# A GpSimd iota between one indirect DMA and the next, in a graph layer with segment maximum

## The chip, the cores and the metric

The kernel runs on one core of a Trainium2 chip. A core has five engines with instruction streams of their own: TensorE (PE in the profile; its weight loads are PEld), VectorE (DVE), ScalarE (ACT), GpSimd (POOL) and SyncE (SP), which here only issues DMAs. They meet at semaphores. All DMAs of the core, whoever issues them, are carried out by its 16 DMA engines. The metric is the device time in microseconds of one execution, lower is better.

## The reference

There are 6250 nodes with 256 features (`x`) and 100,000 edges, each with a source and a destination; the edges come sorted by destination. With the linear maps theta and phi, an edge from s to d has

```python
theta_x = (x_dst - x_src) @ theta_w.T + theta_b
phi_x = x_src @ phi_w.T + phi_b
e = jax.nn.relu(theta_x + phi_x)
out = jax.ops.segment_max(e, dst, num_segments=x.shape[0])
```

A node without edges gets 0. Then `x + out` is normalised over the 256 features: mean taken off, divided by the root of variance + 1e-5.

The maps can be taken apart: the edge's value is A(d) + B(s), with A = x theta_w.T and B = x (phi_w - theta_w).T + both biases. A depends on the destination alone, so a node needs the maximum of B over its sources, and then max(A + that, 0). What remains is matrix work on 6250 rows and, for every edge, the fetching of a row of B (1 KB) and a maximum.

## The kernel before, in words

The nodes are cut into two parts. Part 1 is the first 2154 nodes, part 2 the last 4096 (32 tiles of 128).

*B.* At the start x is loaded in 13 pieces, transposed on TensorE (L669), copied out on ScalarE (L671), multiplied (L675), the bias added on VectorE (L678), and the rows of B are stored to `b_rows` in HBM by DMAs on ScalarE's queue (L693).

*Part 1, by gathers.* Its edges are laid on 128 partitions in chunks of 275. In step t a gather fetches, for each partition, the row of B of that chunk's edge t: one indirect DMA on GpSimd of 128 rows of 1 KB, with its 128 offsets in a column in SBUF. Eight steps make a group with a tile `g` of its own; a ring of seven such tiles (`RING = 7`) lets GpSimd run ahead. VectorE runs through a group's steps (L722): the maximum of the new row with the former one, the former capped to minus infinity where a new node begins. SyncE then stores the group to `maxima_1` (L726). Five of the first groups (`of_x`) gather rows of x instead, while B is not ready, and multiply them on the spot. There are 35 groups, 40 + 235 gathers.

*Part 2, by matmuls in parts ("chunks").* B's rows are cut in 17 slots of up to three blocks of 125 rows. For each slot and each of four chunks of 1024 nodes, at most one source per node and slot is chosen on VectorE (`choice`). A part of (slot, chunk) then loads the wanted row numbers from HBM (L945, SyncE), makes one-hot matrices from them on VectorE (L949) and ScalarE (L951, L952), multiplies them with the slot's rows, split in two float32r terms (L934, L935), on TensorE into PSUM (L959, 24 matmuls of 128 x 512 for a whole part), and VectorE takes the maximum into `acc` (L970; in the first slot ScalarE copies, L968). There are 68 parts. To find a node's sources, 33 short gathers (L475) fetch 640 destinations and then, for each of 32 tile columns, 36 sources a partition; these come early and need what ScalarE counts at L628 and VectorE turns into `begin_i` (L632).

*The left-over list.* Edges of part 2 that no slot took are squeezed into a list of 240 steps (`list_pieces`, L980 to L1040) and gathered as in part 1: 30 groups, 240 gathers, the same ring, L722 and a store to `maxima_2`.

*The end.* `rows_of` gathers the maxima by place (49 gathers), loads x, computes A on TensorE (L1071 to L1077), takes the maximum with `acc` for part 2 (L1086, L1087), adds and applies relu (L1088, L1091); `normalise` squares and scales on ScalarE (L1104, L1111) and stores.

*What sets the order.* The order is written out by hand in the code. Each engine works through its instructions in this order and waits where a semaphore isn't there yet. After two groups for each pair of slots, and a stretch in which the list is squeezed, the loops issue a group of gathers and then 1.2 parts (`PACE`), so the stream of VectorE mixes the L722 steps of gathered groups with L949 and L970 of parts. Between the two lists stands `heads_1`, which repairs the first rows of the chunks with two indirect DMAs (L832, L834) that wait for the stores of part 1.

All gathers but those two go through two helpers:

```python
    def gather(to, table, offsets):
        nc.gpsimd.indirect_dma_start(
            out=to, out_offset=None, in_=table, in_offset=bass.IndirectOffsetOnAxis(ap=offsets, axis=0)
        )
```

`gather` is L467, its DMA L468; `gather_run` is L472, its DMA L475. The helper `iota(t, step, base, per_partition)` (L458, L459) writes an arithmetic sequence along the columns of a tile on GpSimd.

Of the kernel before, what the change touches and what calls it, by code (L numbers as in the profile page):

```python
# [36 lines left out]
FP = mybir.dt.float32  # L37
# [11 lines left out]
P = 128  # L49
# [14 lines left out]
SLOT = 512  # L64
DVE_HOTS = 1
PACE = 1.2
LOWEST = -1.0e30
ABSENT = 1 << 14
MAGIC = 12582912.0
# [8 lines left out]
def flat(t, offset, ap):  # L78

    return bass.AP(tensor=t.tensor, offset=t.offset + offset, ap=ap)  # L80
# [325 lines left out]
def gnn_kernel(ctx: ExitStack, tc: tile.TileContext, x, src, dst, theta_w, theta_b, phi_w, phi_b, out):  # L406
# [27 lines left out]
    const = ctx.enter_context(tc.tile_pool(name="const", bufs=1))  # L434
# [23 lines left out]
    def iota(t, step, base, per_partition):  # L458
        nc.gpsimd.iota(  # L459
            t,  # L460
            pattern=[[step, t.shape[1]]],
            base=base,
            channel_multiplier=per_partition,
            allow_small_or_imprecise_dtypes=True,
        )

    def gather(to, table, offsets):  # L467
        nc.gpsimd.indirect_dma_start(  # L468
            out=to, out_offset=None, in_=table, in_offset=bass.IndirectOffsetOnAxis(ap=offsets, axis=0)
        )  # L470

    def gather_run(to, table, offsets):  # L472

        n = to.shape[1]
        nc.gpsimd.indirect_dma_start(  # L475
            out=to,
            out_offset=None,
            in_=flat(table, 0, [[n, EDGES // n], [1, n]]),
            in_offset=bass.IndirectOffsetOnAxis(ap=offsets, axis=1),
        )  # L480


    src_1 = const.tile([P, T1], I32, name="src_1")
# [6 lines left out]
    def gather_group(i, table):  # L490
        t0, n = groups[i]
        if i not in ring_tiles:
            ring_tiles[i] = gathered.tile([P, STEPS, D], FP, name="g")
        for k in range(n):
            gather(ring_tiles[i][:, k, :], table, src_1[:, t0 + k : t0 + k + 1])
# [75 lines left out]
    lowest_rows = search.tile([P, 2 * D], FP, name="lowest_rows")  # L571
    nc.vector.memset(lowest_rows, LOWEST)
    nc.sync.dma_start(maxima_1[NONE_1 : NONE_1 + 1, :], lowest_rows[0:1, :D])
# [35 lines left out]
    index = body.enter_context(tc.tile_pool(name="index", bufs=1))  # L609
    dst_w = index.tile([P, WINDOW], I32, name="dst_w")  # L610
    gather_run(dst_w, dst_list, edge0_i)
    for i in of_x[X_BEFORE:]:
        gather_group(i, x)
# [10 lines left out]
    for j0 in range(0, TILES + 1, BATCH):  # L624
        j1 = min(j0 + BATCH, TILES + 1)
        for j in range(j0, j1):
            junk = index.tile([P, WINDOW], BF, name="junk")
            nc.scalar.activation(  # L628
                junk, local, AF.Sign, bias=halves[:, j : j + 1], scale=-1.0, accum_out=sums[:, j : j + 1]
            )  # L630
        nc.vector.tensor_scalar(begin[:, j0:j1], sums[:, j0:j1], 0.5, 0.5 * WINDOW, op0=ALU.mult, op1=ALU.add)
        nc.vector.tensor_scalar(begin_i[:, j0:j1], begin[:, j0:j1], edge0, None, op0=ALU.add)  # L632
        for j in range(j0, min(j1, TILES)):
            gather_run(table_i[:, j, :], src_list, begin_i[:, j : j + 1])
# [127 lines left out]
    def node_place(j):  # L762
        cols = columns[:, j // Q1, :]
        hot = work.tile([P, P], FP, name="hot_1")
        nc.vector.tensor_scalar(hot, cols, low[:, j : j + 1], None, op0=ALU.is_ge)
        nc.vector.scalar_tensor_tensor(hot, cols, high[:, j : j + 1], hot, op0=ALU.is_lt, op1=ALU.mult)
        pp = misc()
        nc.tensor.matmul(pp[:, : T1 + 2], hot, ids_1[:, 1:], start=True, stop=True)
        for i in range(2):
            junk = work.tile([P, T1], BF, name="junk_1")  # L770
            nc.scalar.activation(
                junk, pp[:, :T1], AF.Sign, bias=upper[:, i, j : j + 1], scale=-1.0, accum_out=signs[:, i, j : j + 1]
            )
        nc.scalar.copy(origin[:, j : j + 1], pp[:, T1 + 1 : T1 + 2])
# [147 lines left out]
    raw = slots.tile([P, KB, D], FP, name="raw", bufs=1)  # L922
    nc.vector.memset(raw, LOWEST)
    terms_of = {}
# [119 lines left out]
    def group_2(t0):  # L1044
        g = gathered.tile([P, STEPS, D], FP, name="g")
        for k in range(STEPS):
            gather(g[:, k, :], b_rows, list_src[:, t0 + k : t0 + k + 1])
        run(2, g, STEPS, caps_2, t0, maxima_2t)


    def rows_of(part, tiles, ps_tile):
# [11 lines left out]
        for k, j in enumerate(tiles):  # L1063
            gather(m[:, k, :], maxima, places[:, j : j + 1])
# [77 lines left out]
    while groups_1:  # L1142
        group_1(groups_1.pop(0))
        if todo:
            node_place(todo.pop(0))
        pace += PACE
        while pace >= 1.0:
# [13 lines left out]
    while lists:  # L1161
        group_2(lists.pop(0))
        pace += PACE
        while pace >= 1.0:
# [61 lines left out]
```

## Time and profile before

| | |
|---|---|
| time, median of 3 runs | 1137.29 us (1129.62 to 1144.01) |
| profiled execution | 1127.47 us, span 1125.6 us |
| mean granted TensorE clock | 0.788 |
| gathers of the 256-feature rows (L468) | 235 + 240 + 49 + 40, mean 1184, 986, 961, 964 ns |
| short gathers (L475) | 33, 944 ns |
| POOL busy | 640.3 us |
| DVE busy | 630.7 us, of which L722 244.3 and L970 155.5 |
| PE busy | 651.4 us, of which L959 444.9 |
| DMA | 195.61 MB, mean 174 GB/s |

The durations come from one profiled execution. A row of the timeline gives start and duration in us, the engine, the line, the operation, out<-in, how many were merged, and in brackets how long the engine stood idle before and what ended that. A row of waits gives who waited for whom, us in total, how many times, and the longest. "issue" means that the engine waited for nothing that the profile shows; "remote" means that the semaphore was raised by something that the profile could not name. Matmul ends are modelled. [...] The row of a stage gives, for each engine, busy us and the number of instructions, then the granted clock, the mean busy share of the DMA engines and GB/s.

### The profile page before, as it was taken

How to read it: one execution, taken by the hardware profiler on the slowest of the kernel's cores; microseconds unless marked ns; L12 is line 12 of the kernel's file. 1: busy time of each engine (PE TensorE's matmuls, PEld its weight loads, DVE VectorE, ACT ScalarE, POOL GpSimd, SP SyncE). 2: the span in 40 equal slices, each digit the busy share in tenths (PEclk: the TensorE clock that was granted, in tenths of full speed). 3: DMA queues.
4: the chain of work that ended last, by engine and by line, in shares of the span. 5: the costliest groups of instructions: out<-in, count | busy, mean ns of one | idle time of the engine just before them, and what ended most of it. 6: DMA issues, size and time to landing. Idle time of an engine off the chain costs nothing. (4 is left out here: it accounts for less than half of the span.)

```text
span 1125.6 us, 9291 instructions
## 1 busy us (share of the span) xinstructions
PE 651.4 (58%) x2557; PEld 503.6 (45%) x2557; DVE 630.7 (56%) x1309; ACT 429.2 (38%) x680; POOL 640.3 (57%) x622
## 2 busy tenths in 40 slices
PE   0466893585147403295829328578185785986273
PEld 0355783364135302173607216456164664764262
DVE  1221693799978621184758118276165584994164
ACT  0256220564114210075655105276254463830175
POOL 6735377488888777554524754667555756204500
PEclk9888996787668756596959757889586977988696
DMA  6445365477455645264738627566275665735222
GB/s 213 128 138 165 113 193 179 140 254 238 169 173 190 201 144 166 77 221 128 229 122 290 188 81 226 165 220 213 85 238 182 219 202 189 240 144 215 80 99 92
DMA packets 63082, 195.61 MB, mean 174 GB/s; under 512 B 14071, under 2 KB 22795, under 8 KB 53515
## 3 DMA queue, kind: packets, MB, share of 16 engines
q1 hardware_dynamic: 32207, 112.01, 28.3%
q0 software_dynamic: 28272, 75.14, 23.2%
q10 hardware_dynamic: 2540, 7.75, 1.8%
q8 instruction: 23, 0.38, 0.1%
q14 instruction: 40, 0.33, 0.1%
HBM read 114.27 MB, written 81.38 MB: 174 GB/s over the span
## 5 line engine op out<-in xcount | busy, mean ns | idle before, releaser
L959 PE MATMUL ps_f<-hot,terms 128*128 128x512 f32 x1600 | 444.9, 436 | 293.7 <-DVE hot L949 123.0
L959 PEld LDWEIGHTS ps_f<-hot,terms 128*128 128x128 f32 x1600 | 334.6, 213 | 392.5 <-issue 222.9
L468 POOL DMA_INDIRECT g<-b_rows,src x235 | 278.3, 1184 | 118.1 <-issue 67.7
L468 POOL DMA_INDIRECT g<-b_rows,list_src x240 | 236.6, 986 | 148.2 <-issue 72.3
L970 DVE TENSOR_TENSOR acc<-acc,ps_f 128x1024 f32<-128x1024 f32 x128 | 155.5, 1215 | 252.5 <-remote 228.7
L951 ACT ACTIVATE hot<-want,minus_row 128x1024 fp32r<-128x1024 f16 x132 | 146.1, 1145 | 323.3 <-remote 200.3
L722 DVE SCALAR_TENSOR_TENSOR g<-g,caps 128x256 f32<-128x256 f32 x513 | 244.3, 478 | 27.5 <-DMA g<-b_rows,src 9.7
L952 ACT ACTIVATE hot<-hot 128x1024 fp32r<-128x1024 f32 x132 | 133.9, 1050 | 0.4
L675 PE MATMUL ps_b<-weights,x_t 128*128 128x256 f32 x356 | 94.1, 421 | 55.0 <-ACT x_t L671 43.0
L468 POOL DMA_INDIRECT g<-maxima,place x49 | 47.1, 961 | 109.3 <-issue 62.0
L675 PEld LDWEIGHTS ps_b<-weights,x_t 128*128 128x128 f32 x356 | 72.9, 211 | 73.5 <-ACT x_t L671 48.2
L1077 PE MATMUL ps_e<-weights,x_t 128*128 128x256 f32 x128 | 37.4, 440 | 39.2 <-ACT x_t L1073 37.3
L671 ACT COPY x_t<-ps_xt 128x512 f32<-128x512 f32 (+1 forms) x45 | 24.9, 577 | 76.3 <-remote 31.1
L949 DVE TENSOR_SCALAR hot<-want,row_id 128x1024 fp32r<-128x1024 f16 x68 | 50.9, 748 | 1.3 <-ACT hot L952 1.3
L475 POOL DMA_INDIRECT table_i<-src_list,begin_i x32 | 30.2, 944 | 34.0 <-DVE begin_i L632 24.5
L468 POOL DMA_INDIRECT g<-in_x_dram,src x40 | 38.5, 964 | 15.9 <-issue 11.3
L1077 PEld LDWEIGHTS ps_e<-weights,x_t 128*128 128x128 f32 x128 | 25.9, 213 | 47.1 <-ACT x_t L1073 41.2
L678 DVE TENSOR_TENSOR b_sb<-ps_b,bias 128x512 f32<-128x512 f32 (+1 forms) x25 | 16.7, 677 | 52.3 <-PE ps_b L675 22.9
L1104 ACT ACTIVATE squares<-g,r 128x256 bf16<-128x256 f32 x49 | 24.3, 498 | 47.7 <-issue 39.8
L628 ACT ACTIVATE junk<-local,halves 128x640 bf16<-128x640 f32 x33 | 27.4, 830 | 32.1 <-DVE b_sb L678 16.3
L1087 DVE TENSOR_TENSOR g<-g,ps_e 128x512 f32<-128x512 f32 (+1 forms) x17 | 11.1, 655 | 48.7 <-PE ps_e L1086 23.7
L1073 ACT COPY x_t<-ps_e 128x512 f32<-128x512 f32 (+1 forms) x17 | 9.4, 553 | 61.0 <-PE ps_e L1071 38.3
(194 smaller groups left out, 511.1 us busy)
## 6 DMA issues: line engine op xcount, KB each, us to landing
maxima<-g SPq DMA_DIRECT2D x64, 1024.0 KB
want<-chosen_rows SPq DMA_DIRECT2D x68, 256.0 KB
x_q<-in_x_dram SPq DMA_DIRECT2D x12, 512.0 KB
b_rows<-b_sb ACTq DMA_DIRECT2D x12, 512.0 KB
raw<-b_rows SPq DMA_DIRECT2D x16, 336.0 KB
g<-in_x_dram SPq DMA_DIRECT2D x5, 1024.0 KB
out_dram<-g SPq DMA_DIRECT2D x5, 1024.0 KB
g<-b_rows,list_src POOLq DMA_INDIRECT x240
```

Of the source, the lines that this page charges most:

```text
L468: nc.gpsimd.indirect_dma_start(out=to, out_offset=None, in_=table, in_offset=bass.IndirectOffsetOnAxis(ap=offsets, axis=0))
L475: nc.gpsimd.indirect_dma_start(out=to, out_offset=None, in_=flat(table, 0, [[n, EDGES // n], [1, n]]), in_offset=bass.IndirectOffsetOnAxis ...
L628: nc.scalar.activation(junk, local, AF.Sign, bias=halves[:, j : j + 1], scale=-1.0, accum_out=sums[:, j : j + 1])
L671: nc.scalar.copy(x_t[:, :n], ps[:, :n])
L675: nc.tensor.matmul(ps[:, i, :], x_t[:, i, k, :], weights[:, 1, k, :], start=(k == 0), stop=(k == KC - 1))
L722: nc.vector.scalar_tensor_tensor(g[:, k, :], last[part], caps[:, t : t + 1], g[:, k, :], op0=ALU.min, op1=ALU.max)
L949: nc.vector.tensor_scalar(hot[:, b, :], want, row_id[:, b : b + 1], None, op0=ALU.is_equal)
L951: nc.scalar.activation(hot[:, b, :], want, AF.Abs, bias=minus_row[:, b : b + 1], scale=1.0)
L952: nc.scalar.activation(hot[:, b, :], hot[:, b, :].bitcast(FP), AF.Relu, bias=1.0, scale=-1.0)
L959: nc.tensor.matmul(ps[:, w : w + 512], terms[:, part, b, h * P : (h + 1) * P], hot[:, b, w : w + 512], start=(i == 0), stop=(i == n - 1),)
L970: nc.vector.tensor_tensor(to, to, ps, op=ALU.max)
L1077: nc.tensor.matmul(a[:, i, :], x_t[:, 2 * i + c, :], weights[:, 0, c, :], start=(c == 0), stop=(c == KC - 1))
```

## The change

A tile of 128 x 144 float32 of its own, `pause`, is made in SBUF. Behind the indirect DMA in each of the two helpers GpSimd fills it with 0, 1, 2, ... 143 in every partition. Nothing reads it. The two indirect DMAs of `heads_1` are outside the helpers and get no iota behind them.

```diff
+PAUSE = 144
...
+    pause = const.tile([P, PAUSE], FP, name="pause")
+
     def gather(to, table, offsets):
         nc.gpsimd.indirect_dma_start(
             out=to, out_offset=None, in_=table, in_offset=bass.IndirectOffsetOnAxis(ap=offsets, axis=0)
         )
+        iota(pause, 1, 0, 0)
 
     def gather_run(to, table, offsets):
 
@@ -478,6 +483,7 @@
             in_=flat(table, 0, [[n, EDGES // n], [1, n]]),
             in_offset=bass.IndirectOffsetOnAxis(ap=offsets, axis=1),
         )
+        iota(pause, 1, 0, 0)
```

## The prediction

> **What bounds the kernel now.** I read the page's totals first, then the table by stages, then the timelines of GpSimd and TensorE in one stage, then the waits.
>
> ```profile
> span 1125.6 us, 9291 instructions
> PE 651.4 (58%) x2557; PEld 503.6 (45%) x2557; DVE 630.7 (56%) x1309; ACT 429.2 (38%) x680; POOL 640.3 (57%) x622
> ```
>
> No engine is near full, and the busy shares hide two things. The first is in the timeline of GpSimd:
>
> ```profile
> 465.80 0.95 POOL L468 DMA_INDIRECT g<-b_rows,src  x1 [0.30 <-issue]
> 467.06 0.94 POOL L468 DMA_INDIRECT g<-b_rows,src  x1 [0.30 <-issue]
> 468.30 0.95 POOL L468 DMA_INDIRECT g<-b_rows,src  x1 [0.30 <-issue]
> 488.23 1.71 POOL L468 DMA_INDIRECT g<-b_rows,src  x1 [18.98 <-DVE hot L766]
> ```
>
> A gather counts 0.95 us as busy, but the next starts 1.25 us after it: each has 0.30 us of its own that is not counted. With it GpSimd's 597 gathers hold the engine for about 640 + 597 x 0.30 = 820 us of 1126. From 143 to 977 us (493 gathers, 834 us) it stands still for only about 150 us beyond these gaps, waiting for VectorE, as in the last line, or for a store. So GpSimd is the nearest thing to a bound.
>
> The second: in the table by stages (time, then busy time and number of instructions of PE, PEld, DVE, ACT, POOL; clock; DMA share; GB/s) TensorE almost stops in some stretches.
>
> ```profile
> 230.00:290.00 60.00, 41.61 (x158) 31.99 (x156) 58.70 (x137) 31.66 (x36) 49.33 (x36) 0.84 0.72 246
> 395.00:415.00 20.00, 0.00 (x0) 0.00 (x0) 0.02 (x1) 0.00 (x0) 15.13 (x16) 0.50 0.48 157
> 452.00:470.00 18.00, 6.04 (x12) 3.47 (x12) 0.51 (x2) 0.00 (x0) 13.24 (x14) 0.50 0.36 103
> 488.00:507.00 19.00, 18.55 (x81) 14.67 (x79) 15.28 (x29) 11.92 (x21) 14.61 (x14) 1.00 0.78 257
> 507.00:522.00 15.00, 4.26 (x8) 1.82 (x8) 0.32 (x1) 3.79 (x8) 9.55 (x10) 0.64 0.39 114
> 980.00:1000.00 20.00, 17.95 (x78) 14.51 (x77) 19.75 (x32) 12.47 (x12) 0.00 (x0) 0.98 0.54 201
> ```
>
> The DMA engines are not full there (share 0.36 to 0.48, less than where TensorE runs well). What is special is that gathers follow each other every 1.25 us. TensorE's timeline shows the change within one such stretch:
>
> ```profile
> 499.09 5.83 PE L959 MATMUL ps_f<-hot,terms 128*128 128x512 f32 x24
> 511.60 0.59 PE L959 MATMUL ps_f<-hot,terms 128*128 128x512 f32 x1 [1.73 <-issue]
> 514.43 0.59 PE L959 MATMUL ps_f<-hot,terms 128*128 128x512 f32 x1 [0.82 <-issue]
> ```
>
> 24 matmuls take 5.83 us, 0.24 us each; after some 16 gathers in close order one starts every 1.4 us, and it waits for nothing that the profile shows. I call this the crawl. It ends when GpSimd pauses: the last gathers before GpSimd's waits ended at 469.2, 519.4, 667.7, 809.5 and 953.4 us; VectorE got its PSUM tile at 476.9, 522.9, 674.2, 813.7 and 952.2 (the next at 957.2), mostly 3.5 to 7.5 us later. VectorE pays:
>
> ```profile
> DVE acc L970 <- remote: 228.7, 21, 24.4
> POOL g L468 <- DVE g L722: 44.5, 9, 13.1
> POOL g L468 <- DVE hot L766: 37.1, 3, 19.0
> ```
>
> So the middle works in turns: gathers fill the ring of seven tiles while TensorE and VectorE crawl; the ring is full and GpSimd stops; the others catch up; the gathers go on.
>
> **The change.** It removes and moves nothing. It adds 597 iotas of 128 x 144 f32 on GpSimd (564 behind L468, 33 behind L475; none behind the two at L832 and L834), no DMA, no buffer that others use. An iota waits for nobody; behind it on GpSimd stands the next gather, and for that VectorE (L722).
>
> *What one costs.* The nearest rows:
>
> ```profile
> 23.88 0.18 POOL L459 IOTA halves<- 128x33 f32 x1
> 23.99 0.63 POOL L459 IOTA columns<- 128x128 f32 x3
> 24.57 0.23 POOL L459 IOTA ids<- 128x1 f32 x2
> 124.06 0.35 POOL L459 IOTA local<- 128x240 f32 x1
> ```
>
> From start to start 33 columns took 0.11 us and 128 took (24.57 - 23.99) / 3 = 0.193, so 0.0009 us a column and 0.21 us for 144. The high end is the last row, an iota that follows a gather: 0.35 for 240, less 96 columns, 0.27. The low end is zero, if it fits under the 0.30 us gap. Against that: begin_i (L632) ends at 70.40 and the gather that waited for it starts at 70.67. The gap comes after the wait too, so it is the gather's own preparation and runs in series. I take 0.21: a gather every 1.46 us.
>
> *What it should bring.* Where gathers came more slowly, TensorE did not crawl: 36 in 60 us from 230 to 290 (one per 1.67 us) with VectorE full, 14 in the 19 us from 488 (one per 1.36) with TensorE full, but crawling in the 15 us after it (one per 1.25 at the end). I read that as a backlog that fills after 15 to 30 us of gathers at 1.25 to 1.35 us and drains in a few us. Two stretches size it: crawl after about 16 us at 0.8 gathers per us (488 to 507, the ones after 605 and 822 similar) and after about 30 us at 0.74 (143 to 174) give a drain of about 0.68 per us, a limit near 1.47 us. That is an estimate from two points. With 1.46 us, and longer where VectorE delays gathers (the gathers of part 1 took 1184 ns in the mean, 0.95 us where nothing delays them), I expect the crawl mostly gone, though with no margin.
>
> *A rule against it.* The Trainium skill, SBUF — State Buffer, section "Who interferes with whom", says "PE and ACT never wait on anyone", and that nothing on the engines' side contends but VectorE and GpSimd. By it the crawl isn't caused by gathers, the pause buys nothing, and the sum is 1127 plus the pause (rival 1). The rows above, with one matmul per 1.4 us while GpSimd issues and 0.24 us when it doesn't, speak for the link, though not for what carries it; I follow the rows. The same section says that GpSimd and a VectorE operation in a two-port mode exclude each other for the whole instruction. An iota then blocks VectorE at most 0.21 us, in a seventh of the time (0.21 of 1.46): if half of VectorE's 991 instructions of the middle were of that kind, 500 x 0.14 x 0.1 = 7 us, on an engine with over 200 us of idle time. I put in 5 us for both directions together.
>
> *The sum*, against the profiled execution's 1127.47 us (span 1125.6):
> - 0 to 143 us: 33 gathers stand ahead of the one for dst_w, whose landing VectorE awaits for 13.3 us, until 52.16: 33 x 0.21 = +7. In return VectorE's wait of 9.5 us for b_sb, which ended 3.9 us after the last of these gathers, should shrink. The bundles of eight for table_i (+1.7 each) lie under waits for begin_i, but for the last. Together +3. Without the cover: +9.
> - 143 to 977 us: GpSimd's work is 834 - 150 = 684 us. The pauses add 493 x 0.21 = 104. Of the waits I keep 20: the row pass for heads (23.4, 4.1 and 3.5 us at L832 to L834, about 12 when VectorE isn't late) and stores that must land (12.3, about 8). With 5 for the port: 684 + 104 + 20 + 5 = 813, so -21. Late next is GpSimd itself; VectorE has about 510 us of work in it and TensorE about 490.
> - 977 to 1126 us: 24 gathers in close order from 1025.8 cost 24 x 0.21 = +5; ScalarE's wait until 1064.2, again a crawl, should lose about 10. Together -5.
>
> 1127.5 + 3 - 21 - 5 = 1104. The profiled execution lies 10 us below the median of 1137.29 and near the fastest run; I leave the forecast on its basis.
>
> **The rivals.**
> 1. *Slower: the crawl stays as long as gathers run, whatever their pitch.* Then the ring fills more slowly, the others crawl all that time, and the catching-up afterwards is as long as now: + 104 + 7 + 5, 1243; if waits take up a third of the 104, 1208. I take 1210. For it: the crawl is tied to GpSimd being busy at all, which the iota only increases, the rule above, and that at 1.33 to 1.4 us it did come, only later. Against it: the stretch 230 to 290. It decides against the change where less than about 110 of the 150 us of waits disappear.
> 2. *Half: 1.46 us is at the limit, the crawl comes later and lasts shorter.* About 75 us of waits stay in place of 20: 1104 + 55 = 1159.
> 3. *The pause is hidden in the gap* and nothing changes: pitch 1.25, crawl as before, 1120 to 1140, about 1130. Against it the 0.27 us after L632.
>
> **The numbers.** Forecast 0.53 (1104, own range 1065 to 1140: 0.27 us a pause adds 30, no waits at all and a cheaper pause take 35 off), rival 1 0.22 (1165 to 1245), rival 2 0.15 (1135 to 1180), rival 3 0.10. Two per cent of 1137.29, about what a measurement of this kernel can tell, puts the borders at 1114.5 and 1160. Faster by more: about 0.8 of the first case, 0.42. Slower: most of rival 1 and half of rival 2, 0.29. Between: 0.29. The range 1065 to 1205 leaves out the upper half of rival 1 and the tails.
>
> **What would show it.** In the changed profile the gather rows should be 1.46 us apart with iotas of about 0.25 us between; VectorE's wait for acc should fall from 229 to under 60 us; GpSimd's waits for VectorE from over 100 to under 20; TensorE's clock should rise in the middle, since it no longer idles. GpSimd's idle time after 222 us tells the cases apart: near nothing is the forecast, over 100 us is rival 1, a pitch of 1.25 is rival 3. The forecast is wrong if the crawl depends on GpSimd's being busy rather than on gathers per time, or if the iota costs more than 0.27 us next to a gather.

## The result and the profile after

The changed kernel takes 1261.01 us in the median (4 runs, 1258.77 to 1263.68) against 1140.65 us for the kernel before (4 runs, 1129.62 to 1158.63): 1.109 times as long, 95% interval 1.100 to 1.118. Slower by a tenth, where 1104 us was forecast with a range up to 1205.

The page of the changed kernel opens so; the last two lines are groups (busy time and mean ns of one, idle time before it and what ended most of that):

```profile
span 1257.0 us, 9882 instructions
PE 661.6 (53%) x2557; PEld 509.3 (41%) x2557; DVE 636.2 (51%) x1309; ACT 430.3 (34%) x680; POOL 778.7 (62%) x1219
...
L976 DVE TENSOR_TENSOR acc<-acc,ps_f 128x1024 f32<-128x1024 f32 x128 | 155.4, 1214 | 266.5 <-remote 206.8
L460 POOL IOTA pause<- 128x144 f32 x597 | 165.6, 277 | 38.0 <-DMA g<-in_x_dram,src 1.0
```

The iotas are there, 597 of them at 0.28 us, and no other engine has more instructions than before. (Lines after the helpers are six higher: L976 is L970 of the kernel before, L472 and L480 are L468 and L475.) GpSimd's timeline shows what the forecast had not considered:

```profile
105.21 13.07 POOL L460 IOTA pause<- 128x144 f32 x41
...
149.27 21.43 POOL L460 IOTA pause<- 128x144 f32 x55
...
198.84 10.97 POOL L460 IOTA pause<- 128x144 f32 x34
...
219.04 0.95 POOL L472 DMA_INDIRECT g<-b_rows,src  x1 [0.30 <-issue]
220.29 1.58 POOL L472 DMA_INDIRECT g<-b_rows,src  x1 [0.30 <-issue]
221.88 7.49 POOL L460 IOTA pause<- 128x144 f32 x21
```

**The iotas do not stand between the gathers.** Only among the gathers of x at the start does one follow one. Then come 26, 34, 41 and 32 iotas ahead of the four bundles of eight gathers for `table_i`, 68 more ahead of the first gather of part 1, and 10 to 34 between groups of eight gathers that still follow each other every 1.25 us. After 520 us none is left, and the crawl is back as it was. Three rows of TensorE's timeline, then VectorE's longest waits in 0 to 520 us, then the longest in 520 to 1257 us:

```profile
738.20 7.74 PE L965 MATMUL ps_f<-hot,terms 128*128 128x512 f32 x29
746.18 0.40 PE L965 MATMUL ps_f<-hot,terms 128*128 128x512 f32 x1 [0.24 <-issue]
763.65 3.73 PE L965 MATMUL ps_f<-hot,terms 128*128 128x512 f32 x8 [17.07 <-issue]
```

```profile
DVE g L728 <- issue: 67.7, 15, 8.3
DVE g L728 <- DMA g<-b_rows,src: 54.5, 35, 10.6
DVE source L860 <- DMA table_i<-src_list,begin_i: 38.9, 1, 38.9
```

```profile
DVE acc L976 <- remote: 206.8, 17, 24.0
```

Before 520 us no wait of VectorE for `acc` on something unnamed is left. In the first 534 us of the kernel before this was VectorE's longest:

```profile
DVE acc L970 <- remote: 85.6, 5, 24.4
```

In its place VectorE waits for gathered rows (L728; 9.7 us on that DMA before) and for `table_i` (2.7 us before). After 520 us all 206.8 us of the crawl's wait are there.

The gathers' landmarks, first to last start, of the kernel before and then of the changed one:

```profile
L468 POOL DMA_INDIRECT g<-b_rows,src x235: 942/947/7447, 143.0 to 534.3; - x118
```

```profile
L472 POOL DMA_INDIRECT g<-b_rows,src x235: 942/949/2721, 177.3 to 644.3; - x118
```

So of the 131 us between the two spans 34 arise before part 1, 76 in it (391 to 467 us), and 21 behind it, where no iota stands. For those 21 us I have no reason; the kernel before alone spread over 29 us in its four runs.

### The profile page after: what moved, and what is told of

The parts are those of the page before. It is cut to its first block, busy times and chain, and to the rows that moved or that the text cites. A ratio compares the mean times of both kernels' runs of the same rounds, so it can differ in the third digit from the quotient of the medians.

```text
span 1257.0 us, 9882 instructions
## 1 busy us (share of the span) xinstructions
PE 661.6 (53%) x2557; PEld 509.3 (41%) x2557; DVE 636.2 (51%) x1309; ACT 430.3 (34%) x680; POOL 778.7 (62%) x1219
## 5 line engine op out<-in xcount | busy, mean ns | idle before, releaser
L965 PE MATMUL ps_f<-hot,terms 128*128 128x512 f32 x1600 | 453.6, 441 | 414.9 <-DVE hot L955 144.7
L472 POOL DMA_INDIRECT g<-b_rows,list_src x240 | 238.1, 992 | 172.8 <-issue 72.0
L728 DVE SCALAR_TENSOR_TENSOR g<-g,caps 128x256 f32<-128x256 f32 x513 | 244.7, 479 | 136.3 <-issue 72.2
L472 POOL DMA_INDIRECT g<-b_rows,src x235 | 250.3, 1065 | 95.9 <-issue 75.7
L976 DVE TENSOR_TENSOR acc<-acc,ps_f 128x1024 f32<-128x1024 f32 x128 | 155.4, 1214 | 266.5 <-remote 206.8
L460 POOL IOTA pause<- 128x144 f32 x597 | 165.6, 277 | 38.0 <-DMA g<-in_x_dram,src 1.0
L472 POOL DMA_INDIRECT g<-maxima,place x49 | 47.2, 964 | 110.8 <-DMA maxima<-g 52.5
L1083 PE MATMUL ps_e<-weights,x_t 128*128 128x256 f32 x128 | 40.7, 471 | 36.9 <-ACT x_t L1079 36.2
L472 POOL DMA_INDIRECT g<-in_x_dram,src x40 | 38.7, 967 | 8.9 <-issue 6.8
L480 POOL DMA_INDIRECT table_i<-src_list,begin_i x32 | 30.3, 947 | 10.3 <-issue 10.3
```

Source lines behind the costliest of these rows:

```text
L460: nc.gpsimd.iota(t, pattern=[[step, t.shape[1]]], base=base, channel_multiplier=per_partition, allow_small_or_imprecise_dtypes=True,)
L472: nc.gpsimd.indirect_dma_start(out=to, out_offset=None, in_=table, in_offset=bass.IndirectOffsetOnAxis(ap=offsets, axis=0))
L480: nc.gpsimd.indirect_dma_start(out=to, out_offset=None, in_=flat(table, 0, [[n, EDGES // n], [1, n]]), in_offset=bass.IndirectOffsetOnAxis ...
L728: nc.vector.scalar_tensor_tensor(g[:, k, :], last[part], caps[:, t : t + 1], g[:, k, :], op0=ALU.min, op1=ALU.max)
L965: nc.tensor.matmul(ps[:, w : w + 512], terms[:, part, b, h * P : (h + 1) * P], hot[:, b, w : w + 512], start=(i == 0), stop=(i == n - 1),)
L976: nc.vector.tensor_tensor(to, to, ps, op=ALU.max)
```

## Experiments

The kernels of one set of runs ran on one chip beside the kernel before, so ratios hold within a set. That proved necessary: **the kernel before took 901 to 914 us in seven sets and 1108 to 1159 us in four**, the first comparison among them, with nothing in between. The forecast rests on a profile of the second kind. I call the two "without" and "with the crawl". Whether it is the chip or something around it can't be told: one chip number appeared with both.

Theory A: the forecast's mechanism is right and only the place of the iotas was wrong. Theory B: a pause costs its length and the crawl stays. Theory C: the loss is the time of the clumps.

**1. Iotas that really stand between the gathers** (labels *between_72*, *_144*, *_288*, by columns). Each iota is tied behind its own gather in the issue order of GpSimd's queue; the code has no other change:

```diff
-        nc.gpsimd.indirect_dma_start(
+        one = nc.gpsimd.indirect_dma_start(
...
-        iota(pause, 1, 0, 0)
+        with tc.issue_after(one.ins):
+            iota(pause, 1, 0, 0)
```

All but 17 of the 597 then stand behind their gathers; those 17 stand together ahead of the first gather for `table_i`. The other instructions of GpSimd keep their order in every tied kernel. On the other engines the compiled order moves a little with the size: of VectorE's 1309 instructions none stands elsewhere than in the kernel before with 1 column, 4 with 72, 5 with 108, 90 with 144 and 44 with 288 (of the 2557 matmuls 10 with 144, 1 with 288, else none).

> The same 597 iotas of 144 columns, but each is held back on GpSimd until its own gather has been issued, so that in the two gather phases one stands between each two gathers (checked in the order of the queue: 235 pairs of gather and iota in part 1, 240 in the list). In the changed kernel the first 40 gathers, which did have an iota between them, started 1.40 us apart (0.96 + 0.28 + 0.16). Theory A (the forecast's mechanism was right and only the place of the iotas was wrong): with 1.40 us a gather the crawl comes much later or not at all, VectorE waits for acc under 80 us, time 1060 to 1120 us. Theory B (any pause on GpSimd costs its length, the crawl stays as long as gathers run): acc waits stay above 180 us, 1127 + 493 x 0.15 + 7 = about 1208 us, at least 1180.

> As the run with 144 columns held back, with 72 columns: gathers about 1.33 us apart. Theory A: the crawl comes later than with 1.25 us but comes, acc waits of 80 to 200 us, 1085 to 1130 us. Theory B: 1127 + 493 x 0.08 + 5 = about 1170 us.

> As the run with 144 columns held back, with 288 columns: gathers about 1.53 us apart. Theory A: no crawl at all, acc waits under 40 us; GpSimd is then the bound of the middle, 684 + 493 x 0.28 + 25 = 847 us against 834 before, so about 1135 us (1110 to 1150). Theory B: 1127 + 493 x 0.28 + 13 = about 1278 us.

Measured: 1.0935 (1.089 to 1.098), 1.0388 (1.035 to 1.043) and 1.1586 (1.154 to 1.163) times the kernel before, 907.05 us here: 993, 944 and 1052 us. Taken alone this looks like theory B, but the kernel before at 907 us fits neither theory's starting point.

**2. A profile of the kernel before on such a chip.**

> The kernel before, unchanged, for a profile. On the chip of the last four runs it took 907 us against 1137 us on the first chip. Theory E: what is missing there is the crawl; its profile will show TensorE at about 0.24 us a matmul while gathers follow each other every 1.25 us, and almost no wait of VectorE for acc (under 20 us against 229). Rival F: something else is faster there (a higher clock, quicker DMAs), and the matmuls of the stretches with close gathers still start over 1 us apart.

Theory E holds. 911.66 us; the group of `acc`, then TensorE's and GpSimd's timelines:

```profile
L970 DVE TENSOR_TENSOR acc<-acc,ps_f 128x1024 f32<-128x1024 f32 x128 | 155.7, 1216 | 8.1 <-PE ps_f L959 7.8
```

```profile
407.02 11.50 PE L959 MATMUL ps_f<-hot,terms 128*128 128x512 f32 x48
```

```profile
413.11 0.96 POOL L468 DMA_INDIRECT g<-b_rows,src  x1 [0.31 <-issue]
414.37 0.95 POOL L468 DMA_INDIRECT g<-b_rows,src  x1 [0.30 <-issue]
415.62 0.95 POOL L468 DMA_INDIRECT g<-b_rows,src  x1 [0.30 <-issue]
```

48 matmuls at 0.24 us while gathers start every 1.25 us. Rival F falls. The wait for `acc` is 8 us in place of 252. From the first to the last gather of a row of B 701 us pass (832 with the crawl), before them 123 (143), after them 86 (150): the crawl costs this kernel 216 us, and a good part of that in the first and the last stretch.

**3. The changed kernel without the crawl, and its early clumps alone.** *first_250* keeps the iota behind the first 250 calls of `gather` (and behind the 33 of `gather_run`):

```diff
...
-        iota(pause, 1, 0, 0)
+        count[0] += 1
+        if count[0] <= FIRST:
+            iota(pause, 1, 0, 0)
```

> The changed kernel, unchanged, beside the kernel before. On the chip of the last runs, theory C (the cost is the clumps: 597 iotas at 0.347 us from start to start, 207 us, of which part lies under waits) gives some 100 to 150 us over the kernel before, as on the first chip (+120). Where the chip has no crawl, GpSimd has less idle time for the clumps to hide in: 907 + 140 = about 1045 us. The 597 small iotas left in clumps cost 93 us on it.

> The changed kernel with an iota behind the first 250 calls of gather only (and behind the 33 of gather_run): in the queue this leaves exactly the clumps ahead of the second group of part 1 (26, 34, 41 and 32 ahead of the four bundles for table_i, 55 ahead of rank, 37 more), and takes out the 314 later iotas, those that stand between the groups of part 1. Theory C: in the changed profile the first gather of part 1 was 34 us late, so about +35 us (25 to 45); the other 314 iotas make up the rest, 80 us or more. Rival G: the early clumps delay only what is late anyway, under +15 us, and all the loss is made between the groups of part 1.

Measured: changed kernel 1070.61 us (about 1045 was expected), 1.176 (1.172 to 1.181) times the 909.29 us before; *first_250* 969.85 us, 1.066 (1.062 to 1.070). The first and last gathers of part 1 in the kernel before, *first_250* and the changed kernel, all without the crawl (L474 and L472 are L468 of the kernel before):

```profile
L468 POOL DMA_INDIRECT g<-b_rows,src x235: 942/956/3192, 123.3 to 470.5; - x118
```

```profile
L474 POOL DMA_INDIRECT g<-b_rows,src x235: 942/949/3194, 177.5 to 528.5; - x118
```

```profile
L472 POOL DMA_INDIRECT g<-b_rows,src x235: 942/949/2819, 177.5 to 627.9; - x118
```

The iotas ahead of part 1 cost 54 us, in both kernels to 0.1 us. (The expectation of 35 was taken from a profile whose start the crawl had already delayed by 20.) Of the 283 iotas of *first_250* 267 are executed, since 16 stand in the branch that sorts. The other 330 stand in clumps inside part 1: 347 us grow to 450, +103, and without them to 351, +4. At 0.346 us from iota to iota (the mean in the changed kernel's clumps) 330 take 114. So nearly all of this clump time comes through to the end, theory C. Rival G falls. Another order of the rest of the program is no rival here: in both kernels 29 of VectorE's 1309 instructions, three of ScalarE's and one matmul stand elsewhere than in the kernel before, and *first_250*, which has them too, loses only those 4 us in part 1 and none behind it.

Beside the profile with the crawl: there the changed kernel starts part 1 at 177.3 us, as without. What the clumps cost is the same; the crawl of the kernel before, 20 us there and 44 us in part 1 (391 against 347), is gone while they last (but for some 10 us behind the first 16 gathers in a row) and comes back when they are used up (part 1 is 467 us long there, 450 without). That difference, 20 and 44 - 17 us, is what made the loss 34 + 76 in place of 54 + 103.

**4. Small iotas in clumps** (*clumps_1*): `PAUSE = 1` in the changed kernel.

> The changed kernel with 1 column in place of 144, left where the scheduler puts it: the iotas again stand in clumps of 67 to 117 in front of table_i and of 10 to 69 ahead of the first groups of part 1, and none after that. Theory C (what the change cost is the time of the clumps, in front of work that was ready or that others waited for): by start to start of the small iotas in the trace (0.11 us) 597 of them take some 65 us in place of about 207 (0.347 us each), so the loss of 131 us shrinks to about a third: 1160 to 1185 us. Rival D (the loss comes from another order of the rest of the program, which the added instructions brought about): 1230 us or more.

Measured: 1000.03 us, 1.102 (1.098 to 1.107). Theory C's "a third" missed: 93 us against 161 for 144 columns is 58%. A single column takes 0.20 us from start to start in a clump, not 0.11, so 597 take 119 us. And more of them were put ahead of part 1, in clumps of up to 117: its first gather starts at 203.2 us, +80, part 1 itself grows by only 11. By the time alone rival D would not fall: its 1230 us is 93 over 1137, just what was lost. It falls by the order: in this run every instruction of TensorE, VectorE and ScalarE has the place that it has in the kernel before, and of GpSimd's others all but two, and still 93 us are lost.

**5. One phase alone** (*list_144*, *part1_144*): tied iotas of 144 columns behind the 240 gathers of the list, or the 235 of part 1.

> Iotas of 144 columns held between the 240 gathers of the list alone; the first phase (up to the first of these gathers) stays as in the kernel before, as a control within the run. On a chip without the crawl (kernel before about 908 us): GpSimd is the bound of the phase and pays 240 x 0.146 us (1.396 against 1.25 from gather to gather), so +35 us, and the first gather of the list starts as before, near 472 us. On a chip with the crawl (kernel before about 1137 us): Theory A, the phase from the first list gather to the end, 583 us before, shrinks by 40 us or more; Theory B, it grows by 25 to 40 us.

> The counterpart: iotas of 144 columns held between the 235 gathers of part 1 alone. On a chip without the crawl: 347 us for part 1 in the kernel before, of which GpSimd also waits for VectorE now and then; at most 235 x 0.146 = +34 us, less where it waits anyway (20 to 34), and the list phase as before (352 us from first to last gather). On a chip with the crawl: Theory A, part 1 (391 us before, first to last gather) shrinks by 15 us or more, the list phase stays at 433 us; Theory B, part 1 grows by 20 to 35 us.

Both on chips without the crawl: 948.33 against 911.48 us, 1.042 (1.035 to 1.048), and 945.14 against 908.56, 1.040 (1.032 to 1.047). That is +37 and +37 where +35 and at most +34 were expected: within the noise, GpSimd pays each pause in full, in both phases. Neither was run with the crawl.

**6. The same iotas where there is a crawl.** Nothing in the kernels is changed; the tied kernels were run again, and one with a single column and one with 108 added.

> The kernel with an iota of 144 columns held between each two gathers, once more, because the two chips of the runs so far show no crawl (the kernel before takes 907 and 909 us on them, 1137 on the first chip). Where the kernel before takes about 1137 us here, Theory A gives 1060 to 1120 us and Theory B 1180 us or more. Where it takes about 908 us, the outcome of the first such run repeats: 1.09 to 1.10 times the kernel before, GpSimd's gathers 1.40 us apart.

> An iota of a single column held between each two gathers. In the run with clumps of such iotas, where one stood between two gathers of x the gathers started 1.28 us apart (0.96 + 0.14 + 0.16, and 0.02), against 1.25 without: the iota uses up half of the 0.30 us after a gather. On a chip without the crawl: 597 x 0.03 = +18 us at most, 908 + 5 to 20. If the 0.30 us after a gather could take an iota in whole, nothing. On a chip with the crawl (kernel before about 1137 us): Theory A gives little, since 1.28 us is still below the rate at which the crawl was seen to come: within 30 us of the kernel before.

> Iotas of 144 columns held between each two gathers (gathers 1.40 us apart), hoped for on a chip with the crawl, such as that of the last run. There (kernel before 1110 to 1145 us): Theory A (the crawl comes from gathers following each other too closely, and 0.15 us more between them takes most of it away): 1060 to 1115 us, VectorE's wait for acc under 100 us. Theory B (the crawl stays as long as gathers run, whatever their distance): 1180 us or more, acc waits above 180 us. Between them, 1115 to 1180 us: the crawl shrinks by about what the pauses cost. Elsewhere (kernel before about 908 us): 1.09 to 1.10 times the kernel before.

> Iotas of 288 columns held between each two gathers (1.52 us apart). On a chip with the crawl: Theory A, no crawl is left (acc waits under 40 us) and the time is that of the chips without a crawl, GpSimd's own, 1050 to 1080 us; Theory B, 1240 us or more. Elsewhere: 1.16 times the kernel before.

> As in the run before, for a chip with the crawl (kernel before 1110 to 1145 us): Theory A, the crawl mostly goes, 1060 to 1115 us, VectorE's wait for acc under 100 us; Theory B, the crawl stays as long as gathers run, 1180 us or more, acc waits above 180 us; between 1115 and 1180 us the crawl shrinks by about what the pauses cost. Elsewhere 1.09 to 1.10 times the kernel before.

> Iotas of 72 columns held between each two gathers: 1.33 us from gather to gather, between the 1.28 us of one column (0.99 times the kernel before on a chip with the crawl) and the 1.40 us of 144 columns (0.89 times). Where the kernel before takes about 1130 us, it tells where between these the crawl ends: 990 to 1020 us if 1.33 us is enough (GpSimd's own time without the crawl is 944 us with this pause), 1080 to 1120 us if the crawl needs 1.40 us. Elsewhere (kernel before about 908 us): 1.04 times the kernel before.

> Iotas of 108 columns held between each two gathers, about 1.365 us from gather to gather, halfway between 72 columns (0.96 times the kernel before where there is a crawl) and 144 (0.89). Without the crawl GpSimd's own time with this pause is about 967 us. Where the kernel before takes about 1130 us: 970 to 1000 us if this pause is enough, which would be the best of all sizes; 1020 to 1060 us if the crawl only fades with the length. Elsewhere (kernel before about 908 us): 1.06 to 1.07 times the kernel before.

| columns | gather to gather | without the crawl | with the crawl |
|---|---|---|---|
| none | 1.25 us | 907 to 911 us | 1124 to 1134 us beside these |
| 1 | 1.27 | not run | 1118.65, 0.994 (0.989 to 0.998) |
| 72 | 1.33 | 943.69, 1.039 | 1075.84, 0.964 (0.929 to 0.999) |
| 108 | 1.37 | 976.78, 1.073 (1.063 to 1.083) | not run |
| 144 | 1.40 | 992.94, 994.83, 993.00: 1.093 to 1.098 | **1008.31, 0.889 (0.886 to 0.891)** |
| 288 | 1.52 | 1052.37, 1052.93: 1.159 | not run |

(Gather to gather is the median of the gathers of rows of B.) With the crawl, 144 columns make the kernel 11% faster. The 72 columns rest on two runs, and their interval nearly reaches 1; 1076 us lies between the two cases expected, close to "needs 1.40 us". Theory A holds, by more than it forecast (1060 to 1115 us); theory B falls. The group of `acc` (L978 here) and GpSimd's timeline in that run, and the table by stages, first of this run and then of the undisturbed kernel before, for a stretch in which the forecast's table had no matmul at all:

```profile
L978 DVE TENSOR_TENSOR acc<-acc,ps_f 128x1024 f32<-128x1024 f32 x128 | 155.2, 1213 | 6.9 <-PE ps_f L967 6.3
```

```profile
436.09 0.96 POOL L472 DMA_INDIRECT g<-b_rows,src  x1 [0.16 <-issue]
437.05 0.28 POOL L460 IOTA pause<- 128x144 f32 x1
437.49 1.15 POOL L472 DMA_INDIRECT g<-b_rows,src  x1 [0.16 <-issue]
```

```profile
395.00:415.00 20.00, 16.71 (x65) 13.24 (x65) 11.87 (x24) 9.50 (x18) 17.70 (x28) 0.90 0.75 231
```

```profile
395.00:415.00 20.00, 16.97 (x75) 13.45 (x74) 16.16 (x29) 12.78 (x22) 15.43 (x16) 1.00 0.80 250
```

The wait for `acc` fell to 7 us, as low as without the crawl, and the time to some 15 us above what the same kernel takes there. With 72 columns 147 of the 229 us that the kernel before waited for something unnamed are left, and some six tenths of the time (1076 against 944 us without the crawl; 1130 against 908 with no pause):

```profile
DVE acc L978 <- remote: 147.1, 18, 20.4
```

So the crawl fades between 1.33 and 1.40 us from gather to gather. That a longer pause would only cost GpSimd time follows from the runs without the crawl (1.159 with 288 columns); with it none was run. The 144-column kernel differs from the 72-column one also in the order of some 90 instructions of VectorE, and no run separates the two. For the distance speaks that the 597 iotas as such do nothing (1 column, 0.994), and that in the changed kernel the crawl came back within the same execution when the clumps between its groups of gathers were used up. Of the sizes run with the crawl, 144 columns is the best, and this tied version beats both kernels there; without the crawl the kernel before beats every version.

## Why the prediction was wrong

- **"A gather every 1.46 us": this step failed.** It took the place of the call in the code for the place in GpSimd's queue. Text ahead of the prediction says that the order is written out by hand and each engine follows it; that is wrong for GpSimd. An iota that waits for nobody and that nobody waits for did not stay where the code has it. The clumps are part of the compiled program, not of one execution: all 66 groups of iotas have the same sizes in the two profiles of the changed kernel, with the crawl and without. They stand hundreds of us ahead of the gathers that the iotas belong to in the code, and in place of separating gathers they held GpSimd back: 34 us before part 1 and 76 in it. The profile of before had shown it: `list_start` is written at the end of `list_pieces` (L1038) and read at 418.2 us (L1040), and its iota runs at

```profile
25.01 0.13 POOL L459 IOTA list_start<- 128x1 f32 x1
```

- **The rivals.** None was that the iotas would not stand where the code has them. Rival 1 (1208 to 1243) is nearest in time, but not in kind: while iotas were issued there was hardly any crawl. Rival 3, hidden in the gap, was half true of an iota between gathers: the 0.30 us after a gather shrink to 0.16.
- **The iota's price.** 0.21 us in series was taken, between 0 and 0.27. Between two gathers it is 0.146 us (1.396 less 1.25); in a clump 0.346. The kernel without the crawl confirms the first: 597 x 0.146 = 87 us, measured 82 to 88.
- **"Backlog", with a limit near 1.47 us.** That crowding of gathers makes the crawl is borne out by the size of the pause (1.27, 1.33, 1.40 us), with the change of order named above. The limit lies lower, between 1.33 and 1.40. A backlog of data it is not: in 395 to 415 us of the crawling profile the last packet of a gather ended 1.46 us (median) after the end of the instruction, in the undisturbed one 2.49 us.
- **"It waits for nothing that the profile shows" and "it ends when GpSimd pauses".** The first holds for one matmul every 1.4 us, but not for the stretches without any; the second holds for some stretches only. In 395 to 415 us TensorE had nothing to start:

```profile
384.82 3.02 PE L959 MATMUL ps_f<-hot,terms 128*128 128x512 f32 x12 [1.13 <-issue]
415.97 2.19 ACT L951 ACTIVATE hot<-want,minus_row 128x1024 fp32r<-128x1024 f16 x2 [28.84 <-remote]
415.97 1.22 DVE L970 TENSOR_TENSOR acc<-acc,ps_f 128x1024 f32<-128x1024 f32 x1 [20.95 <-remote]
```

  By the modelled ends the matmuls are done at 387.84. ScalarE and VectorE, which both wait for TensorE's semaphore, start together 28 us later, at the moment at which the trace records its update. So the "remote" of these waits is TensorE itself: either its matmuls or their signal come late, and modelled ends can't tell which. In this profile of 125 waits of over 1 us that were released by TensorE's semaphore, 53 ended more than 1 us after the last matmul that could have released them, in the undisturbed one none of 88; with tied iotas and the crawl 48 of 116 for 72 columns, and for 144 columns 9 of 79, none by more than 3.7 us. Signals of VectorE and ScalarE are not late so: in the profile of before one of 89, by 1.4 us. And GpSimd did not pause at 415.97: its gathers went on every 1.25 us around it, and its first pause of that stretch is the one at 469.2.
- **The sum.** Set against tied iotas with the crawl (span 1006.1), its three terms were: 0 to 143 us, +3 forecast, -7.5 measured (part 1 starts at 135.5); the middle, 834 to 813 forecast, 774 measured, 39 less, 32 of them because the iota is cheaper (493 x (0.21 - 0.146)); behind it -5 forecast, -54 measured (150.3 to 96.4). The mechanism was right and the sizes short, most in the last stretch, where the crawl was put down as 10 us.
- **GpSimd as nearest to a bound** is right, and fully so without the crawl, where every pause between gathers is paid.
- **The rule of the Trainium skill, SBUF — State Buffer, section "Who interferes with whom"**, "PE and ACT never wait on anyone". Without the crawl the trace agrees (0.24 us a matmul beside gathers every 1.25 us). With it TensorE starts one every 2.1 us (at 767.99, 770.09 and 772.19 us in the changed kernel) or stands still for 17 us, and spreading the gathers ends that. So the rule can't be used as the prediction considered it, to exclude that gathers hold TensorE up; there the measurement decides, and to follow the rows was right. Whether TensorE is held up at SBUF, of which the section speaks, no run shows.

## What to carry to other kernels

Before costing an instruction by its neighbours, look where the trace shows that independent instructions of its kind really ran; what depends on nothing is moved, and a pause must be tied to what it is to separate. A helper instruction on the engine that is the bound is paid in full where the trouble that it should cure is absent, so measure both kernels side by side, more than once. And a clump costs more than its parts: without the crawl the same 597 iotas cost 161 us in clumps and 86 us one by one.

## What was not expected of the hardware

- The crawl belongs to some runs of the program as a whole: 1108 to 1159 us in four sets of runs, 901 to 914 us in seven, same program. What causes it stays open. The packets land as early as ever, but the records of semaphore updates by the gathers' DMAs thin out: in most stretches of 10 us with eight close gathers there are 1 to 3 a gather in the profiles with the crawl, about 16 in those without. They are thinned out (5579 against 9577) also in the tied run in which 144 columns had ended most of the crawl, so the thinning alone does not make it. Every time on record comes from an execution with a recorded span and clock; whether recording has a part in the crawl, no run shows.
- It has a sharp edge: 0.07 us more between gathers (1.33 to 1.40) took the waiting for `acc` from 208 us, named and unnamed, to 7.
- An iota in a clump starts 0.20, 0.26, 0.32 and 0.44 us after the one before for 1, 72, 144 and 288 columns (medians; for 72 and 288 of the one clump of 17 in the tied kernels). A gather behind an iota starts 0.16 us after it, behind a gather 0.30 us.
